# Float32r products of 12-bit parts for scores and queries in a latent-attention layer

## The chip, the core and the metric

The kernel runs on one core of a Trainium2 chip, as one launch. The metric is the device time in microseconds of that launch, the median of several runs. The core has a matrix engine (TensorE, PE in the profile, with its weight loads as PEld), three engines for elementwise work (VectorE or DVE, ScalarE or ACT, GpSimd or POOL), and SyncE (SP), from whose queue nearly all transfers are issued. Matmul results land in PSUM, from where DVE and ACT read them.

## What is computed

One transformer layer on 8 sequences of 512 tokens with 512 features: attention with latent queries and keys (16 heads), then a gated feed-forward block. Cut to what matters:

```python
x = hidden                                        # (8, 512, 512)
a = layernorm(x)
q = rmsnorm(a @ wq_a.T, q_norm_w)                 # latent of 384
q = (q @ wq_b.T).reshape(b, s, 16, 128 + 64)      # per head: q_nope 128, q_pe 64
kv = a @ wkv_a.T
kv_c = rmsnorm(kv[..., :128], kv_norm_w)          # latent of 128
k_pe = rope(kv[..., 128:])                        # 64, shared by all heads
k_nope, v = split(kv_c @ wkv_b.T)                 # per head 128 and 128
scores = (concat(q_nope, rope(q_pe)) @ concat(k_nope, k_pe).T) / sqrt(192)
out = softmax(scores) @ v
x = x + out @ wo.T
y = layernorm(x)
x = x + ((silu(y @ e4m3(gate_w) * gs) * (y @ e4m3(up_w) * us)) @ e4m3(down_w)) * ds
```

All inputs and the output are float32.

## The kernel before

**Folding.** The key projection is folded into the query weights and the value projection into the output weights. `fold_q(h)` multiplies a head's `wqn` and `wkn` and keeps the product, scaled by both norm weights, in SBUF (`wa0` to `wa3`, four heads each); `sum_q` adds the sums of weight blocks that Strassen's scheme needs. So scores need only the 128-wide latent of the keys, and no keys or values per head are made. `fold_o` does the same for the output; those weights go to scratch memory and come back for each later sequence (`wst`).

**Per sequence.** `latents(b)` normalizes the tokens, projects them with `wlr` (a Strassen scheme of its own, `project_two_x`), and transposes the result into `lat`: three blocks of 128 rows of query latent and one of key latent, by 512 tokens. `kpe` holds the rotary keys as two float32r parts, a rounded one and the remainder.

**Per pair of heads.** `project_pe` makes the rotary queries of two heads with three 128x512 float32 matmuls (`qpe_ps`, L659), applies the rotation (`rope`, L442 to L445) and splits the result into float32r parts in `qpe`. `project_two` makes the latent queries `qn` of two heads by a Strassen scheme over the two heads and the two halves of the tokens: eleven 128x256 float32 matmuls (L746) in four stages, with halves copied and added by ACT and DVE (L760 to L782). The first pair is done by `project`, with six full matmuls (L692).

**Per head, four steps.** One step is one `scores(b, h, t)`: 128 queries against 512 keys. One float32 matmul with the latent (L793) and two float32r matmuls with the rotary parts (L795) add into one PSUM tile `sc`. DVE takes the negated maximum `nmax` (L797), ACT the exponential with its sum `den` (L800). One step later DVE inverts `den` (L803) and ACT scales (L804); another step later DVE transposes 32x32 blocks (L169). Every two steps `send` writes the blocks to scratch memory (`way`, L179) and reads them back as the full transpose `prT` (L183). `attend` multiplies `prT` with the values' latent `kvt` (L814), six steps after the last score of its head. `sums` and `output` form the output product of four heads by another Strassen scheme (L860) and add it to `x` on DVE (L864).

**Order.** All of this is written out by hand: `steps` lists the (sequence, head, tile) steps in order, `work[i]` holds what is issued in step `i` beside the scores, and `put(i, f)` adds to it; `at(b, h, t)` gives a step's number. Every engine runs its own instructions in that order. `put_q` places the query projections, 4 to 6 steps before the head that needs them. In each step the loop first issues the transpose of the step before last, then the inverse and the scaling of the last step, then the scores, maximum and exponential of this one, then `work[i]`. While attention runs, the feed-forward weights are rounded to e4m3 in pieces (L73 to L84) and stored.

**PSUM.** The ring `ps_r` has 5 buffers of 128x512 float32, used by `sc`, `av`, projections and transposes in turn; `ps_q` has one for Strassen's sums, `ps_o` two for output products.

**Feed-forward.** It runs after attention, with float32r throughout: `y` and the gated result are split into two parts, and each product takes two matmuls (L267, L1188).

Of the kernel before, what the change touches and what calls it, by code (L numbers as in the profile page):

```python
# [45 lines left out]
P = 128  # L46
# [3 lines left out]
NH = 16  # L50
# [12 lines left out]
RL = RQ + RKV + DR  # L63

# [24 lines left out]
class Layer:  # L89
    def __init__(self, ctx, tc, ins, out):  # L90
# [4 lines left out]
        self.ps_r = ctx.enter_context(tc.tile_pool(name="ps_r", bufs=5, space=PSUM))  # L95
# [4 lines left out]
        self.wlr = self.wp.tile([P, NC, RL], F32, tag="wlr", name="wlr")  # L100
# [7 lines left out]
        self.size = {"wg": 3, "wu": 6, "wd": 4}  # L108
# [8 lines left out]
        ]  # L117

# [16 lines left out]
    def ln_stats(self, x, small):  # L135
# [3 lines left out]
        st = small.tile([P, NT, 6], F32, tag="ln_st", name="ln_st")  # L139
        mv = small.tile([P, NT, 2], F32, tag="ln_mv", name="ln_mv")  # L140
        sd = small.tile([P, NT], F32, tag="ln_sd", name="ln_sd")
        rstd = small.tile([P, NT], F32, tag="ln_rstd", name="ln_rstd")
# [61 lines left out]
    def ffn_parts(self):  # L204
        return (
            self.xp.tile([P, NC, S], F32R, tag="lat", name="yh", bufs=2),
            self.wp.tile([P, NC, S], F32R, tag="wlr", name="yl"),
        )

    def ffn_normed(self, x, small, psum, work):  # L210
# [3 lines left out]
        yh, yl = self.ffn_parts()  # L214
        *stats, mv, rstd = self.ln_stats(x, small)
# [16 lines left out]
    def ffn_normed_blocks(self, x, y, small, work):  # L232
# [3 lines left out]
        yh, yl = self.ffn_parts()  # L236
# [39 lines left out]
    def attention(self):  # L276
        tc, nc, ins, wp, xp = self.tc, self.nc, self.ins, self.wp, self.xp
        with ExitStack() as ctx:
# [4 lines left out]
            ps_q = ctx.enter_context(tc.tile_pool(name="ps_q", bufs=1, space=PSUM))  # L283
# [20 lines left out]
            wlr_sums = wp.tile([P, 3, 2, RL // 2], F32, tag="wlr_sums", name="wlr_sums")  # L304
# [10 lines left out]
            nc.gpsimd.tensor_scalar(knr, knr, SCALE, None, ALU.mult)  # L315
            cs_s = None
            wqp_s, wa_s, wst_s = [], [], {}
# [9 lines left out]
            def load_pe(g):  # L327

                wqp = self.load_w(f"wqp{g}", ins["wqp"][g])
                wqp_s.append(wqp)  # L330

                def times():
                    for r in range(NR):
                        nc.gpsimd.tensor_scalar(
                            wqp[:, r, :], wqp[:, r, :], qnw[:, r : r + 1], None, ALU.mult
                        )

                return times
# [8 lines left out]

            def fold_q(h):


                fold_q_products(h)()

            def fold_q_products(h):

                g, j = divmod(h, G)
# [15 lines left out]

                return evict

            def sum_q(pair):

# [886 lines left out]
```

## Time and profile before

| | |
|---|---|
| median of 3 runs | 2683.82 us (2683.11 to 2685.96) |
| span of the profiled execution | 2680.7 us, 30590 instructions |
| profiled execution's own time beside its span | not given by the page; the median is 3.1 us above the span |
| granted TensorE clock | 1.000 of full speed |
| transfers | 433.51 MB, mean 162 GB/s |
| first and last score matmul | 38.9 and 2127.7 us |

The profile is of one execution. Its page gives the busy time of each engine, the span in 40 slices, and groups of instructions by line, engine and tile, with the mean time of one and the idle time of the engine just before them with what ended it. Matmuls overlap in their pipeline and their ends are modelled, so the distance from one start to the next says what a matmul costs. A float32 matmul of the program leaves two records, a float32r matmul one.

### The profile page before, as it was taken

What the parts mean: (1) busy time and instruction counts of PE and PEld (TensorE: products, weight loads), DVE (VectorE), ACT (ScalarE), POOL (GpSimd) and SP (SyncE); (2) the same over time, 40 slices, a digit from 0 to 9 for tenths busy, and PEclk for the clock granted to TensorE, in tenths of its full rate; (3) what the DMA queues carried; (4) which work ended last, traced back from release to release, by engine and by line L of the source; (5) the groups of instructions that cost most, each with busy time, mean ns of one, the idle gap of its engine ahead of it and who ended that gap; (6) DMA issues with size and microseconds to landing.
All of it is one profiled execution on the core that took longest, in us unless ns stands there. A gap on an engine that the chain in (4) does not pass through costs nothing.

```text
span 2680.7 us, 30590 instructions
## 1 busy us (share of the span) xinstructions
PE 2668.3 (100%) x9782; PEld 1820.0 (68%) x9782; DVE 1506.2 (56%) x3369; ACT 1272.8 (47%) x2675; POOL 655.9 (24%) x754
## 2 busy tenths in 40 slices
PE   9999999999999999999999999999999999999999
PEld 5566666666666666666666666666666688888887
DVE  5655566656666666566666666666555543333332
ACT  4454554555455545555545454555555433333332
POOL 3342222222222222222222222222111122222222
PEclk9999999999999999999999999999999999999999
DMA  4665565555655555565555555655565641111110
GB/s 124 219 197 172 173 202 182 180 178 187 188 178 179 198 180 177 181 205 176 174 192 187 181 171 189 204 173 167 183 213 190 204 159 65 63 64 66 64 63 20
DMA packets 266561, 433.51 MB, mean 162 GB/s; under 512 B 30112, under 2 KB 193312, under 8 KB 264864
## 3 DMA queue, kind: packets, MB, share of 16 engines
q1 hardware_dynamic: 262080, 426.64, 49.0%
q10 hardware_dynamic: 4320, 4.92, 0.7%
q8 instruction: 78, 1.28, 0.2%
q14 instruction: 83, 0.68, 0.1%
HBM read 256.33 MB, written 175.11 MB: 161 GB/s over the span
## 4 chain that ended last, share of the span: by engine, by line
PE 92%; ACT 3%; DVE 3%; DMA 1%; issue 0%; SPq 0%; ACTq 0%; POOL 0%; DVEq 0%; POOLq 0%
PE av L814 16%; PE sc L793 14%; PE sc L795 8%; PE u_ps L860 7%; PE pd L1188 7%; PE pg L267 6%; PE qn_two L746 6%; PE pu L267 6%; PE qpe_ps L659 6%; PE v_ps L860 4%; PE qn_ps L746 3%; PE z_ps L860 2%; PE lr_u L548 2%; PE lr_z L548 1%; DMA way<-block 1%; ACT pr L804 1%
## 5 line engine op out<-in xcount | busy, mean ns | idle before, releaser
L804 ACT ACTIVATE pr<-pr,den 128x512 f32<-128x512 f32 x512 | 369.9, 722 | 658.0 <-DVE den L803 652.5
L797 DVE TENSOR_REDUCE nmax<-sc 128x1 f32<-128x512 f32 x512 | 347.8, 679 | 317.0 <-PE sc L795 315.7
L795 PE MATMUL sc<-kpe,qpe 128*128 128x512 f32 x1024 | 525.8, 594 | 0.0
L793 PE MATMUL sc<-lat,qn 128*128 128x512 f32 x1024 | 523.0, 592 | 0.5 <-ACT qn L776 0.5
L814 PE MATMUL av<-prT,kvt 128*128 128x512 f32 x1024 | 460.5, 592 | 0.6 <-issue 0.3
L800 ACT ACTIVATE pr<-sc,nmax 128x512 f32<-128x512 f32 x512 | 346.7, 677 | 157.1 <-DVE nmax L797 156.8
L169 DVE STREAM_TRANSPOSE block<-pr 128x512 f32<-128x512 f32 x512 | 359.4, 702 | 16.6 <-DMA way<-block 12.5
L795 PEld LDWEIGHTS sc<-kpe,qpe 128*128 128x128 f32 x1024 | 194.5, 190 | 244.9 <-issue 244.1
L814 PEld LDWEIGHTS av<-prT,kvt 128*128 128x128 f32 x1024 | 193.7, 189 | 196.2 <-issue 185.5
L445 POOL TENSOR_TENSOR roped<-roped,rope_sw 128x512 f32<-128x512 f32 x72 | 91.7, 1274 | 809.0 <-DVE rope_sw L444 792.7
L793 PEld LDWEIGHTS sc<-lat,qn 128*128 128x128 f32 x1024 | 192.2, 190 | 78.9 <-issue 45.5
L1171 POOL TENSOR_TENSOR fl<-fuse,fh 128x512 fp32r<-128x512 f32 x96 | 126.5, 1318 | 381.9 <-ACT fh L1170 381.9
L1167 DVE SCALAR_TENSOR_TENSOR fuse<-pu,us,gate 128x512 f32<-128x512 f32 x96 | 71.9, 750 | 193.9 <-PE pu L267 189.0
L659 PE MATMUL qpe_ps<-lat,wqp 128*128 128x512 f32 x384 | 175.3, 592 | 0.7 <-issue 0.7
L1188 PE MATMUL pd<-wd,fh 128*128 128x512 f32 (+1 forms) x396 | 150.5, 383 | 0.0
L1188 PE MATMUL pd<-wd,fl 128*128 128x512 f32 (+1 forms) x396 | 150.5, 383 | 0.0
L267 PE MATMUL pu<-yh,wu 128*128 128x512 f32 x384 | 150.1, 391 | 0.4 <-ACT gate L1165 0.4
L267 PE MATMUL pg<-yh,wg 128*128 128x512 f32 x384 | 150.0, 391 | 0.0
L78 POOL TENSOR_TENSOR raw<-raw,q_m 128x256 f32<-128x256 f32 x72 | 63.9, 887 | 349.7 <-DVE q_m L76 349.7
L267 PE MATMUL pu<-yl,wu 128*128 128x512 f32 x384 | 149.4, 389 | 0.0
L267 PE MATMUL pg<-yl,wg 128*128 128x512 f32 x384 | 149.4, 389 | 0.0
L1165 ACT ACTIVATE gate<-pg,gs 128x512 f32<-128x512 f32 x96 | 66.0, 689 | 174.0 <-PE pg L267 173.5
(169 smaller groups left out, 4162.0 us busy)
## 6 DMA issues: line engine op xcount, KB each, us to landing
way<-block SPq DMA_DIRECT2D x256, 512.0 KB, 3.1
prT<-way SPq DMA_DIRECT2D x1024, 128.0 KB, 2.8
wst<-wst_d SPq DMA_DIRECT2D x56, 512.0 KB, 4.5
wst<-wst_d SPq DMA_DIRECT2D x56, 384.0 KB, 3.9
x<-in_hid SPq DMA_DIRECT2D x60, 256.0 KB, 3.4
x<-x SPq DMA_DIRECT2D x16, 512.0 KB, 4.4
out<-o SPq DMA_DIRECT2D x31, 256.0 KB, 2.0
wst_d<-wst SPq DMA_DIRECT2D x8, 896.0 KB, 4.6
```

The source lines that it names most:

```text
L169: self.nc.vector.transpose(out[:, :, :, i : i + Q].rearrange("p c k i -> p k c i"), x.rearrange("p (k c j) -> p k c j", c=NQ, j=Q),)
L267: self.nc.tensor.matmul(ps, self.ffn_w[name, i][:, c * P : (c + 1) * P], y[k][:, c, :], start=c == 0 and k == 0, stop=c == NC - 1 and k == 1,)
L659: nc.tensor.matmul(ps, wqp_s[g][:, r, pj * P : (pj + 1) * P], lat[:, r, :], start=r == 0, stop=r == NR - 1)
L746: nc.tensor.matmul(to, m, n, start=start and k == 0, stop=stop and k == len(terms) - 1, skip_group_check=True,)
L793: nc.tensor.matmul(sc, qn[:, q], lat[:, NR, :], start=True, stop=False)
L795: nc.tensor.matmul(sc, qpe[:, h % 2, q], kpe[:, part, :], start=False, stop=part == 1)
L797: nc.vector.tensor_reduce(nmax, sc, AX.X, ALU.max, negate=True)
L800: nc.scalar.activation(pr, sc, AF.Exp, bias=nmax, accum_out=den)
L804: lambda: nc.scalar.activation(pr, pr, AF.Identity, scale=den),
L814: nc.tensor.matmul(av, kvt[:, kt, :], prT[:, :, :, kt, :], start=kt == 0, stop=kt == NT - 1)
L860: nc.tensor.matmul(got[name][:, t, :], ops[p][left][:, t * P : (t + 1) * P], w[:, p, right, :], start=first and t == 0 and p == 0, stop=la ...
L1188: nc.tensor.matmul(pd, f[:, i, t * P : (t + 1) * P], w["wd", i][:, cols], start=i == 0 and f is fh, stop=i == NI - 1 and f is fl,)
```

## The change

- Scores: `qn` and the key latent (`latk`) are each kept as three float32r parts: a rounded high part, the remainder, and a difference of the two. The float32 matmul L793 becomes three float32r matmuls. They go into two PSUM tiles: `mid` takes the product of the differences and the two rotary products (L763, L765), `sc` the products of the high parts and of the remainders (L767). ACT copies `mid` to `pr` with a scale (L771), DVE adds `sc`, scales and takes the minimum in one instruction (`tensor_tensor_reduce`, L773), and the exponential reads the result with scale -1.
- Query projections: latent queries and rotary queries of a pair of heads are made by the same function `project_q`, nine float32r matmuls for each of three outputs (L703, L710), again in two PSUM tiles, joined by an ACT copy (L707) and a DVE instruction (L714). `project_two`, `sum_q`, `sum_latents` and the Strassen halves are gone. `project` splits `qn` into parts on ACT, POOL and DVE (L722 to L724).
- The query weights' three parts are made once, in the first sequence (`weight_parts`), stored to scratch memory (`wq_d`), and loaded again for each pair of each later sequence, in three pieces; a ring of two buffers holds them.
- The query latent's parts (`latq`, one buffer) come from `transpose_q`; the key latent has its own `transpose_kv`.
- `ps_r` has 6 buffers, and `ps_q` is gone. The first product of the query's rotation moves from DVE to POOL (L457). The reading back of `prT` is issued one turn later. In the loop, the scaling of the last step (`between`) is issued on ACT between the copy of `mid` and the exponential. The output's third step is cut in two, and some work is placed in other steps. The rotary cast L681 is gone; the second difference goes to DVE as two 64-row instructions (L750, L751). Gate weights are loaded in two pieces of six.

The diff, cut to its core:

```diff
-        self.ps_r = ctx.enter_context(tc.tile_pool(name="ps_r", bufs=5, space=PSUM))
+        self.ps_r = ctx.enter_context(tc.tile_pool(name="ps_r", bufs=6, space=PSUM))
...
+            def weight_parts(p, j, w4, engine=nc.gpsimd):
+                parts = wq_s[0, p]
+                hi, lo, mid = (parts[:, k, :, j * P : (j + 1) * P] for k in range(3))
+                nc.scalar.activation(mid, w4, AF.Identity, scale=DOWN)
+                nc.scalar.activation(hi, w4, AF.Identity, scale=DOWN * T)
+                engine.tensor_tensor(lo, w4, mid, ALU.subtract)
+                engine.tensor_tensor(mid, hi, lo, ALU.subtract)
...
+            def load_wq(b, p):
+                def piece(k):
+                    if k == 0:
+                        wq_s[b, p] = wp.tile([P, 3, NR, 3 * P], F32R, tag="wq", name="wq", bufs=2)
+                    nc.sync.dma_start(wq_s[b, p][:, k].bitcast(F32), self.wq_d[p][:, k].bitcast(F32))
...
+                    hi, lo, mid = (latq[0][:, k, :, t * P : (t + 1) * P] for k in range(3))
+                    nc.scalar.activation(hi, pt, AF.Identity, scale=DOWN)
+                    nc.vector.tensor_tensor(lo, pt, hi, ALU.subtract)
+                    nc.vector.scalar_tensor_tensor(mid, hi.bitcast(F32), -ONE_T, pt, ALU.mult, ALU.add)
...
+            def project_q(b, pair, k):
+                w = wq_s[b, pair]
+                latq = state["latents", b][0][0]
+                cols = slice(k * P, (k + 1) * P)
+                ps, mid = (ps_r.tile([P, S], F32, tag="r", name=n) for n in ("q_ps", "q_mid"))
                 for r in range(NR):
                     nc.tensor.matmul(
-                        ps, wqp_s[g][:, r, pj * P : (pj + 1) * P], lat[:, r, :], start=r == 0, stop=r == NR - 1
+                        mid, w[:, 2, r, cols], latq[:, 2, r, :], start=r == 0, stop=r == NR - 1
                     )
+                q = hp.tile([P, S], F32, tag="qa", name="qa", bufs=2)
+                nc.scalar.copy(q, mid)
+                for part in range(2):
+                    for r in range(NR):
+                        nc.tensor.matmul(
+                            ps, w[:, part, r, cols], latq[:, part, r, :],
+                            start=part == 0 and r == 0, stop=part == 1 and r == NR - 1,
+                        )
+                nc.vector.scalar_tensor_tensor(q, ps, ONE_T, q, ALU.mult, ALU.add)
+                return q
...
+                def parts():
+                    qn = state["qn", b, h] = hp.tile([P, 3, S], F32R, tag="qn", name="qn")
+                    nc.scalar.activation(qn[:, 0, :], q, AF.Identity, scale=DOWN)
+                    nc.gpsimd.tensor_tensor(qn[:, 1, :], q, qn[:, 0, :], ALU.subtract)
+                    nc.vector.scalar_tensor_tensor(
+                        qn[:, 2, :], qn[:, 0, :].bitcast(F32), -ONE_T, q, ALU.mult, ALU.add
+                    )
...
-                sc = ps_r.tile([P, S], F32, tag="r", name="sc")
-                nc.tensor.matmul(sc, qn[:, q], lat[:, NR, :], start=True, stop=False)
+                mid, sc = (ps_r.tile([P, S], F32, tag="r", name=n) for n in ("mid", "sc"))
+                nc.tensor.matmul(mid, qn[:, 2, q], latk[:, 2, :], start=True, stop=False)
                 for part in range(2):
-                    nc.tensor.matmul(sc, qpe[:, h % 2, q], kpe[:, part, :], start=False, stop=part == 1)
+                    nc.tensor.matmul(mid, qpe[:, h % 2, q], kpe[:, part, :], start=False, stop=part == 1)
+                for part in range(2):
+                    nc.tensor.matmul(sc, qn[:, part, q], latk[:, part, :], start=part == 0, stop=part == 1)
...
-                nc.vector.tensor_reduce(nmax, sc, AX.X, ALU.max, negate=True)
-                nc.scalar.activation(pr, sc, AF.Exp, bias=nmax, accum_out=den)
+                nc.scalar.activation(pr, mid, AF.Identity, scale=1.0 / ONE_T)
+                between()
+                nc.vector.tensor_tensor_reduce(
+                    pr, sc, pr, scale=-ONE_T, scalar=3.0e38, op0=ALU.add, op1=ALU.min, accum_out=nmax
+                )
+                nc.scalar.activation(pr, pr, AF.Exp, bias=nmax, scale=-1.0, accum_out=den)
...
                         def turned(i=i, blocks=blocks, block=block, prT=prT, t=t):
+                            while on_way and i < len(steps) - 2:
+                                on_way.pop(0)()
                             blocks()
                             if t % 2:
                                 on_way.append(self.send(prT[:, t // 2], block))
-                                while i != len(steps) - 3 and on_way:
-                                    on_way.pop(0)()
+                            while on_way and i == len(steps) - 1:
+                                on_way.pop(0)()
```

## The prediction

> **What bounds the kernel now.** I read the page first: the busy shares and the 40 slices.
>
> ```profile
> PE 2668.3 (100%) x9782; PEld 1820.0 (68%) x9782; DVE 1506.2 (56%) x3369; ACT 1272.8 (47%) x2675; POOL 655.9 (24%) x754
> ```
>
> TensorE is busy for the whole span. The windows view says whether that holds in both stages; after the window come PE, weight loads, DVE, ACT, POOL, the granted clock, the DMA share and GB/s.
>
> ```profile
> 820.00:1080.00 260.00, 259.79 (x896) 167.74 (x895) 161.68 (x377) 136.40 (x298) 63.77 (x77) 1.00 0.58 186
> 2158.00:2681.00 523.00, 518.72 (x2311) 430.12 (x2309) 195.03 (x340) 163.44 (x270) 126.45 (x96) 1.00 0.20 70
> ```
>
> In attention (scores start from 38.9 to 2127.7 us, so 261 us a sequence and 4.08 us for each of its 64 score steps) PE leaves 0.2 us idle in 260; DVE is at 62%, ACT at 52%, POOL at 25%. A busy PE is no proof of necessary work, so I need the price of each matmul. Durations of pipelined matmuls overlap (rows say 592 ns), so prices are start-to-start. The chain of waits, cut to a stretch where it stays on PE, adds them up:
>
> ```profile
> 1005.72 0.86 PE qn_two L746 x4
> 1006.58 0.86 PE qn_ps L746 x4
> 1007.44 0.86 PE sc L793 x2
> 1008.30 0.47 PE sc L795 x2
> 1008.77 3.44 PE av L814 x8
> 1013.53 2.58 PE qpe_ps L659 x6
> ```
>
> Each float32 matmul leaves two records: one 128x512 product costs 0.86 us, one 128x256 half 0.43. The float32r pair L795 is one record each: 0.47 for two. The feed-forward stage, all float32r, in the timeline gives the steady price: 54 matmuls between these two starts, 12.23 us, 0.2265 each, each with its own weight load and at clock 1.00.
>
> ```profile
> 2299.66 0.39 PE L267 MATMUL pg<-yl,wg 128*128 128x512 f32 x1
> ...
> 2311.89 0.39 PE L267 MATMUL pg<-yl,wg 128*128 128x512 f32 x1
> ```
>
> So three float32r products cost 0.68 against 0.86. The other engines' prices are in the groups by form:
>
> ```profile
> L804 ACT ACTIVATE pr<-pr,den 128x512 f32<-128x512 f32 x512 | 369.9, 722 | 658.0 <-DVE den L803 652.5 <-DMA wo<-in_wo 2.5 <-issue 2.2
> L800 ACT ACTIVATION_READ_ACCUMULATOR pr<-sc,nmax 128x1 f32 x512 | 97.9, 191 | 0.0
> L817 ACT COPY o<-av 128x512 f32<-128x512 f32 x128 | 74.8, 585 | 142.7 <-PE av L814 142.7
> L673 ACT CAST qpe<-roped 128x512 fp32r<-128x512 f32 x64 | 39.6, 619 | 0.3 <-POOL roped L445 0.3
> L797 DVE TENSOR_REDUCE nmax<-sc 128x1 f32<-128x512 f32 x512 | 347.8, 679 | 317.0 <-PE sc L795 315.7 <-DVE den L803 0.3
> L803 DVE RECIPROCAL den<-den 128x1 f32<-128x1 f32 x512 | 63.6, 124 | 5.5 <-ACT pr L800 5.5
> L444 DVE SCALAR_TENSOR_TENSOR rope_sw<-rope_sw,cs 128x512 f32<-128x512 f32 x72 | 49.4, 687 | 0.0
> L641 POOL TENSOR_TENSOR kpe<-roped,kpe 128x512 fp32r<-128x512 f32 x8 | 10.2, 1277 | 1.1 <-ACT kpe L640 1.1
> ```
>
> The long idle entries of ACT and DVE end on each other or on PE: they have room, but each step hands work back and forth.
>
> **PE's part.** Scores: in each of 512 steps one float32 matmul (0.86) becomes three float32r (0.68): -0.1805 x 512 = -92.4 us. Queries: a pair of heads had three rotary matmuls (2.58) and eleven Strassen halves (11 x 0.432 = 4.75), together 7.33; now it has 27 float32r matmuls, 6.12. That is -1.21 x 63 = -76.5, and the first pair, which had nine full matmuls (7.74), gains 1.6. Transposes, attention products, output products and feed-forward keep their counts. Sum: -170.5 us. The granted clock is 1.00 in every window, the all-float32r ones included, so I take no slower matmul. Break-even would be a float32r price of 0.28 us.
>
> **ACT's part.** Each step gains a copy of `mid` out of PSUM (by L817, 585 ns; 512 of them, 299.5 us); each head and pair a copy of `q_mid` (192, 112.3) and each head a rounding to float32r (128 by L673, 79.4). The four half copies of a pair (63 x 4 at 0.3625, 91.4) and one of three rotary casts (39.6) go. Weight parts, first sequence only, add about 48 x 0.47 = 23 (between the 256- and 512-wide copies). Net +383, or +45 for a later sequence: 136 + 45 = 181 of 240 us, 76%.
>
> **DVE's part.** The reduce becomes an add-and-minimum over PSUM and SBUF that also writes its output, plus an accumulator read. No row shows it. Its nearest row is the reduce, 0.68; the two-input reads of PSUM (L864, 0.687) agree. The accumulator read lies between DVE's one-column reciprocal (0.124) and ACT's read (0.191). I take 0.81 in all; the lower bound is 0.68, no read at all; the upper bound is two passes, 2 x 0.679 + 0.191 = 1.55. New: 192 joins of `ps` and `mid` (132.5), 128 third parts of q (by L444, 88), smaller latent parts (40), one more rotary half (43); +66 for the reduce. Gone: 106 for the halves, 43 for the rope product that moves to POOL. Net +221, 27.6 a sequence: 190 of 240, 79%.
>
> One rule speaks against this: the Trainium skill's page "Vector Engine (DVE) Microarchitecture Reference", section "Points that are easy to get wrong", says that a scalar-tensor-tensor with two non-bf16 sources in SBUF runs at half throughput. L444 is that form and took 687 ns, against 674 ns for L443 with a PSUM source, so here the row decides. By the rule the third parts of q would cost about 0.65 us more each, an estimate: 10 us of DVE a sequence.
>
> **POOL's part.** 128 second parts of q (1.28 each by L641, 164), 64 rope products (82), weight and latent parts, less Strassen's sums: about +30 a later sequence, 95 of 240 or 40%. Its results are used a step or more later, 3.75 us, which covers 1.28; without that cover PE would wait up to 1.3 us for each of 128 heads, 164 us.
>
> **Transfers.** Query weights no longer stay resident: 168 loads of 576 KB, 99 MB, in sequences 2 to 8. At the 186 GB/s now moved, 14 MB a sequence lifts the rate to about (48 + 14) MB in 240 us, 260 GB/s. Each load costs SP about 0.4 us of issue, and is queued ahead of `way` and `prT`; the first use comes 9 steps after the first piece (34 us) and 5 after the last (19), against landings of 4 to 5 us for 384 to 512 KB, so it is hidden. `prT` is now issued one turn later, so that SP does not sit on `way`'s landing (787.8 us today); attention products still start six steps after the scores, 22.5 us. From scores to `prT` I count two steps and a transpose (8.2), landing 3.1, issue 1.7, landing 2.8: 16 us. Doubling both landings still fits; nothing, or at most 2 us a head (256 us), which I keep for the range only.
>
> **New waits.** A step's chain is copy 0.585, reduce 0.81, exponential 0.68 and its read 0.19, with 0.04 at each hand-over (the reduce ended at 1006.44, the exponential began at 1006.48): 2.35 us, against 3.75 of PE on average. In ACT's queue the exponential now waits for a reduce that itself waits for a copy just ahead of it; behind it stand the copies that free PE's banks. The old scaling L804 fills most of that gap. The ring `ps_r` has six buffers for 24 tiles in eight steps, two steps of lead, where it had five for about 13, three steps. Some steps carry only a score (1.13 us of PE), and ACT gets two table loads of 1.283 us around each square root; then PE can catch up with its ring. Between 0 and 6 us a sequence, I take 2: 17 us in all, nearer to none, because ACT and DVE both keep a fifth of their time.
>
> **Start.** Before the first score come eight latent-part instructions on DVE (0.55 each, by the 384-wide row L469, 4.4 us), two POOL steps for the key latent and one for q (3 x 1.28); 0 to 12, I take +8.
>
> **Sum.** Span 2680.7 - 170.5 + 8 + 17 = 2535.2. The page gives no total of the profiled run beyond its span; the median of 2683.8 lies 3.1 above that span, so the forecast is 2538 us.
>
> **The rivals.** *ACT and DVE pace the steps.* For it: 76 and 79% busy with a chain each step, and a ring with a third less lead. Against it: 0.7 us of slack a step. If PE waits 0.1 to 0.3 us a step, 51 to 154 us replace the 17: 2572 to 2675.
>
> *Slower: the fused reduce takes two passes* (L773, every step). At 1.55 us DVE's 190 becomes 237 of 240, and with some 0.25 us a step of waiting for copies and reads about 253; 5% more where joins of q bunch makes 265, 25 a sequence above PE's 240, 200 us in place of the 17: about 2721. It decides from about 1.5 us. For it: a second input, an output and an accumulator in one instruction, unseen here. Against it: L864, L444 and L1167, the two-input forms, all took 0.68 to 0.75.
>
> *The price does not carry over:* if float32r matmuls cost 0.28 in attention, as when weight loads (0.19 each) do not hide, the result is no change. Against it: the pair L795 already runs at 0.23.
>
> **How the numbers follow.** The forecast case, PE still the bound (2509 to 2565), 0.57; steps paced by ACT and DVE, 0.30; no change 0.02; slower 0.11. The range 2508 to 2612 holds the first and a little over half of the second. A difference of 0.2%, 5 us, is about what can be told from none: faster 0.87, same 0.02, slower 0.11.
>
> **What would show it.** Right: L763 and L767 starts 0.23 apart, PE near 100% in windows of sequences 2 to 8, the score step at 3.75 to 3.85 us, DVE near 79%, the feed-forward stage still 523 us. Wrong: idle time ahead of `mid` or `q_mid` on PE released by DVE or ACT (the ring), ahead of `av` released by a DMA, or an L773 row far above 0.7 us.

## The result: slower, and the profile after

The changed kernel takes 2754.4 us (median of four runs, 2752.8 to 2758.0) against 2683.5 us beside it: a ratio of 1.0266, with an interval from 1.0251 to 1.028. The forecast was 2538. The profiled execution has a span of 2752.4 us, so 71.7 us were lost where 145 were expected to be won.

The page of the changed kernel: busy time by engine, then PE's busy share and its granted clock in 40 slices.

```profile
PE 2582.6 (94%) x10240; PEld 1911.8 (69%) x10240; DVE 1778.6 (65%) x4021; ACT 1605.5 (58%) x3245; POOL 1005.7 (37%) x943
PE   7899899989998999899999998999999999999999
PEclk8999999999999999999999999999999999999999
```

PE was at 100% and has gaps now, nearly all in the attention stage. The windows view shows the same two stages as before.

```profile
820.00:1080.00 260.00, 239.89 (x926) 173.19 (x927) 192.34 (x444) 167.97 (x348) 98.78 (x93) 0.99 0.75 229
2230.00:2752.00 522.00, 518.62 (x2289) 426.24 (x2287) 200.51 (x337) 161.54 (x269) 125.99 (x96) 1.00 0.20 69
```

In 260 us of attention PE idles for 20 us, and more than that shows when its work is priced. I priced every matmul of the traces start to start, as the prediction did (0.2266 us for a float32r matmul, 0.429 for each of the two records of a 128x512 float32 product). In all, the matmuls come to 2650.7 us before and 2481.9 after: 168.8 us less, where the prediction took 170.5. But from the first score to the last attention product PE spends 16.5 us more than its prices before and 239.1 us more after. That is the whole result: -167 for the matmuls of that stretch, +223 for time in which PE stood or ran slowly, +12 for a later first score (38.9 to 50.7 us), +4 behind the last attention product.

No engine is full, however. The groups by form show what the instructions cost:

```profile
L773 DVE CUSTOM_DVE_ANT_0 pr<-sc,pr 128x512 f32<-128x512 f32 x512 | 345.2, 674 | 72.3 <-ACT pr L771 69.9 <-PE mid L765 0.3
L773 DVE DVE_READ_ACCUMULATOR2_ANT nmax<- 128x1 f32 x512 | 42.0, 82 | 0.0
L771 ACT ACTIVATE pr<-mid 128x512 f32<-128x512 f32 x512 | 300.2, 586 | 75.5 <-PE mid L765 75.2 <-issue 0.2
L714 DVE SCALAR_TENSOR_TENSOR qa<-q_ps,qa 128x512 f32<-128x512 f32 x192 | 132.8, 692 | 279.7 <-ACT qa L707 249.3 <-PE q_ps L710 20.1 <-issue 8.9
L724 DVE SCALAR_TENSOR_TENSOR qn<-qn,qa 128x512 fp32r<-128x512 f32 x128 | 119.0, 930 | 148.5 <-ACT qn L722 147.4
```

The fused reduce took 0.674 us and its accumulator read 0.082, together 0.756: one pass. The durations are as predicted; the new part is the idle time at the end of the lines. Before, the largest wait of DVE in attention was for PE (316 us, L797 in the prediction). The waits view, DVE's and then PE's (us in total, times, longest):

```profile
DVE qa L714 <- ACT qa L707: 249.3, 178, 1.9
DVE qn L724 <- ACT qn L722: 147.4, 74, 3.7
DVE pr L773 <- ACT pr L771: 69.9, 117, 3.2
...
PE u_ps L836 <- DVE x L620: 24.4, 12, 2.4
PE q_mid L703 <- ACT pr L771: 18.7, 9, 2.2
PE av L790 <- ACT pr L771: 16.2, 18, 1.3
PE mid L763 <- DVE qn L724: 15.7, 13, 2.0
PE sc L767 <- DVE nmax L773: 14.2, 20, 1.3
```

DVE waits for ACT, 467 us in these three rows alone, and each of PE's five largest rows names one of the two. The rows of `q_mid` and `av` behind L771 and of `sc` behind L773 are waits for a bank of the ring `ps_r`, which that instruction frees; `mid` behind L724 waits for its operand. The timeline shows one turn of it (start, duration, in brackets the idle time ahead and its end):

```profile
855.57 1.62 PE L703 MATMUL q_mid<-latq,wq 128*128 128x512 f32 x3 [2.15 <-ACT pr L771]
856.98 2.40 PE L710 MATMUL q_ps<-latq,wq 128*128 128x512 f32 x6
...
857.56 0.57 ACT L771 ACTIVATE pr<-mid 128x512 f32<-128x512 f32 x1
...
858.04 0.71 ACT L780 ACTIVATE pr<-pr,den 128x512 f32<-128x512 f32 x1
858.17 0.69 DVE L773 CUSTOM_DVE_ANT_0 pr<-sc,pr 128x512 f32<-128x512 f32 x1 [0.32 <-ACT pr L771]
...
858.91 0.72 ACT L776 ACTIVATE pr<-pr,nmax 128x512 f32<-128x512 f32 x1 [0.16 <-DVE nmax L773]
...
859.63 0.57 ACT L707 COPY qa<-q_mid 128x512 f32<-128x512 f32 x1
860.23 0.69 DVE L714 SCALAR_TENSOR_TENSOR qa<-q_ps,qa 128x512 f32<-128x512 f32 x1 [1.36 <-ACT qa L707]
```

The copy L707 of `q_mid` stands behind the exponential L776 in ACT's queue; the exponential waits for DVE's reduce L773; and next in DVE's queue is the join L714, which waits for L707. So DVE stands for exponential, read and copy, 1.36 us here and 1.40 on average over 178 times. The third part L724 does the same behind the rounding L722, for 74 of the 128 heads. The six matmuls at 856.98 show something else: 2.40 us, where six of them took 1.52 at 1007.71. They ran at half clock: the granted clock was 0.5 from 855.4 to 858.8 us, around the end of a wait of PE of 2.15 us.

### The profile page after: what moved, and what is told of

Its sections match the earlier page's. It is cut to its first block, busy times and chain, and to the rows that moved or that the text cites. A ratio compares the mean times of both kernels' runs of the same rounds, so it can differ in the third digit from the quotient of the medians.

```text
span 2752.4 us, 34226 instructions
## 1 busy us (share of the span) xinstructions
PE 2582.6 (94%) x10240; PEld 1911.8 (69%) x10240; DVE 1778.6 (65%) x4021; ACT 1605.5 (58%) x3245; POOL 1005.7 (37%) x943
## 4 chain that ended last, share of the span: by engine, by line
PE 31%; DVE 7%; ACT 6%; DMA 3%; issue 3%; SPq 1%; POOL 0%; DVEq 0%; ACTq 0%
PE pu L272 6%; PE pd L1178 6%; PE pg L272 6%; PE av L790 3%; DVE block L175 2%; ACT pr L776 2%; PE u_ps L836 2%; PE q_ps L710 2%; ACT pr L780 2%; DMA way<-block 1%; PE mid L765 1%; PE sc L767 1%; PE q_mid L703 1%; PE v_ps L836 1%; DVE pr L773 1%
## 5 line engine op out<-in xcount | busy, mean ns | idle before, releaser
L773 DVE CUSTOM_DVE_ANT_0 pr<-sc,pr 128x512 f32<-128x512 f32 x512 | 345.2, 674 | 72.3 <-ACT pr L771 69.9
L776 ACT ACTIVATE pr<-pr,nmax 128x512 f32<-128x512 f32 x512 | 364.5, 712 | 12.3 <-DVE nmax L773 9.2
L767 PE MATMUL sc<-latk,qn 128*128 128x512 f32 x1024 | 323.6, 396 | 26.2 <-DVE nmax L773 14.2
L771 ACT ACTIVATE pr<-mid 128x512 f32<-128x512 f32 x512 | 300.2, 586 | 75.5 <-PE mid L765 75.2
L765 PE MATMUL mid<-kpe,qpe 128*128 128x512 f32 x1024 | 319.6, 393 | 6.2 <-DVE qpe L751 6.2
L723 POOL TENSOR_TENSOR qn<-qa,qn 128x512 fp32r<-128x512 f32 x128 | 213.5, 1668 | 306.0 <-ACT qn L722 305.5
L714 DVE SCALAR_TENSOR_TENSOR qa<-q_ps,qa 128x512 f32<-128x512 f32 x192 | 132.8, 692 | 279.7 <-ACT qa L707 249.3
L710 PE MATMUL q_ps<-latq,wq 128*128 128x512 f32 x1152 | 306.6, 403 | 0.3 <-DVE nmax L773 0.3
L763 PE MATMUL mid<-latk,qn 128*128 128x512 f32 x512 | 278.5, 544 | 21.8 <-DVE qn L724 15.7
L710 PEld LDWEIGHTS q_ps<-latq,wq 128*128 128x128 f32 x1152 | 226.9, 197 | 51.5 <-DVE nmax L773 0.9
L767 PEld LDWEIGHTS sc<-latk,qn 128*128 128x128 f32 x1024 | 188.8, 188 | 85.4 <-DVE nmax L773 24.9
L765 PEld LDWEIGHTS mid<-kpe,qpe 128*128 128x128 f32 x1024 | 192.7, 189 | 63.3 <-issue 29.0
L82 POOL TENSOR_TENSOR raw<-raw,q_m 128x256 f32<-128x256 f32 x72 | 64.7, 898 | 442.0 <-DVE q_m L80 437.3
L724 DVE SCALAR_TENSOR_TENSOR qn<-qn,qa 128x512 fp32r<-128x512 f32 x128 | 119.0, 930 | 148.5 <-ACT qn L722 147.4
L703 PE MATMUL q_mid<-latq,wq 128*128 128x512 f32 x576 | 177.7, 418 | 34.6 <-ACT pr L771 18.7
```

The lines of the kernel that those rows point to most:

```text
L710: nc.tensor.matmul(ps, w[:, part, r, cols], latq[:, part, r, :], start=part == 0 and r == 0, stop=part == 1 and r == NR - 1,)
L723: nc.gpsimd.tensor_tensor(qn[:, 1, :], q, qn[:, 0, :], ALU.subtract)
L763: nc.tensor.matmul(mid, qn[:, 2, q], latk[:, 2, :], start=True, stop=False)
L765: nc.tensor.matmul(mid, qpe[:, h % 2, q], kpe[:, part, :], start=False, stop=part == 1)
L767: nc.tensor.matmul(sc, qn[:, part, q], latk[:, part, :], start=part == 0, stop=part == 1)
L771: nc.scalar.activation(pr, mid, AF.Identity, scale=1.0 / ONE_T)
```

## The experiments

Two numbers stand beside each run: what PE lost against its prices from the first score to the last attention product, and for how much of that stretch the granted clock was 0.5, both from the trace. Five kernels were run once (e_ring5, e_one_sum, e_q_only, e_scores_only, e_early_start), three twice (e_order_nopool, e_order_one_sum, e_order3_dve), the others four to ten times; runs of one kernel lie within 3.5 us of each other, those of the changed kernel within 5.2, of e_q_late within 6.7 and of e_early_warm within 9.8. The kernel before, run again beside each group, took 2682.0 to 2683.7 us.

| run | us | PE lost | at half clock |
|---|---|---|---|
| before | 2683.5 | 16.5 | 0 |
| after | 2754.4 | 239.1 | 75.1 |
| e_ring5 | 2754.3 | 237.0 | 44.4 |
| e_one_sum | 2722.1 | 206.9 | 102.4 |
| e_q_only | 2702.0 | 95.9 | 54.6 |
| e_scores_only | 2693.0 | 75.8 | 27.3 |
| e_q_late | 2683.3 | 81.9 | 27.3 |
| e_early | 2698.5 | 181.8 | 92.2 |
| e_early_warm | 2683.8 | 169.4 with dummies | 54.6 |
| e_early_start | 2663.9 | 146.8 | 47.8 |
| e_order2 | 2653.6 | 138.7 | 81.9 |
| e_order | 2631.4 | 116.4 | 30.7 |
| e_order_nopool | 2625.9 | 110.6 | 44.4 |
| e_order3_dve | 2628.2 | 112.7 | 34.1 |
| e_order3 | 2621.8 | 106.4 | 23.9 |
| e_order_one_sum | 2589.7 | 72.7 | 27.3 |

Theory A: the order of ACT's and DVE's queues, in which a head's work for q stands behind the step's exponential and reduce, holds PE. Rival B: the PSUM ring `ps_r` is too short for its new tiles. Rival C: DVE and POOL block each other.

**The ring with five buffers.**

```diff
-        self.ps_r = ctx.enter_context(tc.tile_pool(name="ps_r", bufs=6, space=PSUM))
+        self.ps_r = ctx.enter_context(tc.tile_pool(name="ps_r", bufs=5, space=PSUM))
```

> The changed kernel with five instead of six buffers in ps_r. Theory A: PE's lead is not what limits, 2750 to 2785. Theory B: a sixth of the lead gone where the lead is the limit, 2830 or more. Theory C: as A.

2754.3 us, no difference, where B expected 2830 or more: the number of buffers is not what holds PE. The ring is not free of cost, though. PE's largest wait is now for a bank:

```profile
PE av L790 <- DVE nmax L773: 34.3, 27, 2.7
```

In the changed kernel that row is 2.0 us. What the waits added was about made up by 31 us less at half clock (worth at most 15 us, an estimate at half speed), so a sixth of the ring may be worth some 13 us; the equal times hide that by luck. A longer ring was not run.

**One PSUM sum for the scores**, with the old reduction and exponential, without copy, fused reduce and the scale between the sums.

```diff
-                mid, sc = (ps_r.tile([P, S], F32, tag="r", name=n) for n in ("mid", "sc"))
+                sc = ps_r.tile([P, S], F32, tag="r", name="sc")
...
-                nc.scalar.activation(pr, mid, AF.Identity, scale=1.0 / ONE_T)
                 between()
-                nc.vector.tensor_tensor_reduce(
-                    pr, sc, pr, scale=-ONE_T, scalar=3.0e38, op0=ALU.add, op1=ALU.min, accum_out=nmax
-                )
-                nc.scalar.activation(pr, pr, AF.Exp, bias=nmax, scale=-1.0, accum_out=den)
+                nc.vector.tensor_reduce(nmax, sc, AX.X, ALU.max, negate=True)
+                nc.scalar.activation(pr, sc, AF.Exp, bias=nmax, accum_out=den)
```

> All five score matmuls add into one PSUM tile without the scale between the two sums (so the scores are not the reference's); the copy of mid and the fused reduce give way to the old reduce and the exponential from PSUM. PE's matmuls, the query projections and their joins stay. Ring demand falls from 24 to 16 tiles in eight steps, ACT loses 0.58 us a step. Theory A: the waits of the joins behind the exponential stay (1.36 us each), the step's chain loses the copy: 2640 to 2720. Theory B: the ring has its old three steps of lead, 2540 to 2590. Theory C: 2740 or a little less.

2722.1 us. This is 2 us above A's range and far from B's. 300 us of ACT's copies and a third of the ring's tiles are gone, and only 32 us come back: neither ACT's busy time nor the ring is the limit. The two waits of q stay about as they were, as the waits view of this run shows:

```profile
DVE qa L714 <- ACT qa L707: 232.2, 168, 1.9
DVE qn L724 <- ACT qn L722: 172.2, 74, 5.1
```

**The work for q issued ahead of the step's scores.** PE's query matmuls, ACT's copy L707, its rounding and POOL's second part go ahead of the step's copy and exponential; DVE's join and third part stay behind the reduce. Nothing else changes.

```diff
-                put(i + n, plain)
+                early[i + n].append(plain)
...
+                        while early[i]:
+                            early[i].pop(0)()
                         inverse, times, blocks = scores(b, h, t, block, times or (lambda: None))
```

> Same arithmetic; in each step the query matmuls, ACT's copy of q_mid and ACT's and POOL's parts of qn are issued ahead of the step's scores, while DVE's join (L714) and third part (L724) stay behind the reduce, so that neither waits for an ACT instruction queued behind the exponential. Theory A (DVE's queue sets the pace: about 200 us busy plus 62 us waiting for ACT in each sequence of 273): L714's 249 us and L724's 147 us of waiting nearly vanish, PE idles less, 2560 to 2640 us. Theory B (the ring of six PSUM buffers for 24 tiles in eight steps sets the pace): the demand on the ring is the same, 2735 to 2765. Theory C (DVE and POOL block each other): also unchanged, 2735 to 2765.

2698.5 us (ratio to before 1.0061, 1.0045 to 1.0078): 56 us better by order alone. The time lies between the ranges: above A's (2560 to 2640) and below that of B and C. So the order matters, as A says, but not to the extent expected. The waits of L714 and L724 vanish; DVE now waits for the copy of `mid` behind the same ACT work, and PE at a few single places:

```profile
DVE pr L775 <- ACT pr L773: 422.3, 301, 7.8
...
PE q_mid L703 <- issue: 32.0, 7, 4.6
PE u_ps L838 <- DVE x L620: 30.0, 12, 2.8
```

The first PE row is the start of each later sequence; the view names no releaser, but at 845.24 us `q_mid` starts 0.1 us after the last L657 ends. `latq` has one buffer, so its four transposes follow the last head's projection; each passes through ACT and twice through DVE (L655 to L657) before `q_mid` of the next sequence can start. The old kernel had one copy there. The second is the bank that DVE frees late after the latents' products.

**Each half of the change alone.** First q in float32r and the scores in one float32 sum as before:

```diff
-                nc.tensor.matmul(mid, qn[:, 2, q], latk[:, 2, :], start=True, stop=False)
+                nc.tensor.matmul(sc, qn[:, q], latk, start=True, stop=False)
```

> Only the query projections are float32r; scores are one float32 matmul and two float32r in one tile, with the old reduce and exponential, and qn needs no parts. By PE's prices 2683.5 - 78 + 5 = 2611. Theory A: DVE has 24 joins a sequence that wait for ACT, but no third parts and no fused reduce; its queue has room: 2605 to 2640. Theory B: 14 tiles in six buffers, the same, 2605 to 2630. If it is far above, the projections alone carry the loss.

2702.0 us, far above either expectation. PE idles for 56 us in attention, and half of that is one row, seven times at a sequence's start:

```profile
PE q_mid L698 <- issue: 27.5, 7, 4.2
```

The loss was about 10 us for each later sequence, more than twice the 3.9 us of the wait. Then the scores from parts, with q as three float32 matmuls in one sum:

```diff
+                        ps, w[:, 0, r, cols].bitcast(F32), latq[:, 0, r, :].bitcast(F32), start=r == 0, stop=r == NR - 1
```

> The other half of the change: scores as three float32r products in two sums with the copy and the fused reduce, but q as three float32 products of 128x512 in one PSUM sum, copied out by ACT (no joins, no third or second parts of weights and latents); each head still makes its three parts of q. PE: 512 x 0.18 less, a pair of heads 7.74 in place of 7.33: 2683.5 - 92 + 26 = 2617 us without any new wait. Theory 'the queues' ping-pong per head costs the most' (third part L724 waits for ACT behind the exponential): 2650 to 2700. Rival 'the join L714 alone is the wait': 2617 to 2635.

2693.0 us, in the range of the theory named first: its third part of q waits for ACT (225 us; the copy of `mid` is waited for longer, 248). Its largest row on PE is 18.1 us, seven waits of up to 2.8 us at a later sequence's start, for `qpe`. So each half alone loses its gain: q 79 us more on PE than before, against 78 gained; the scores 59 against 66, and 17 us at the start and behind the last product. Neither is "the" cause, and together they lose 223, more than 79 and 59: the losses of the halves don't simply add.

**A sequence's start reordered.** The transposes take three steps in place of four, and the first rotary projection comes one step later; first on the kernel with float32r for q alone, then on e_early.

```diff
-                    first = b > 0 and h == 0
+                    first = 2 * (b > 0 and h == 0)
...
-                    put(at(b - 1, 13, 2) + t, p["transpose_q"], t)
+                    put(at(b - 1, 13, 2) + (t + 1) // 2, p["transpose_q"], t)
```

> Only q in float32r, scores in one float32 sum, and the start of a sequence reordered: the four transposes of the query latents take three steps instead of four, and the first rotary projection of a sequence is issued one step later. In the run without the reordering PE idled 4.1 us once a sequence ahead of that projection, and the loss against the sum of matmul prices was 9.5 us a sequence with the half-clock stretch that followed. Theory 'waits at one place, doubled by the clock gate': the loss goes, 2702 - 7 x (6 to 9.5) = 2636 to 2660, faster than before, and the row q_mid <- issue of 27.5 us vanishes. Rival 'the engines beside PE set the pace': the wait moves to the next place that needs DVE or ACT, 2690 to 2702.

2683.3 us (1.0003, 0.9994 to 1.0012): 19 us better, less than half of the expectation. The wait ahead of `q_mid` is gone, and a new one of 2.2 us ahead of the rotary matmul of the scores has come (15.9 us in all), probably because the parts of `qpe` are now made one step before their use.

> The kernel with ACT's and PE's query work issued ahead of the step's scores (2698.5 us), and in addition the same reordering of a sequence's start. There PE idled 4.74 us at each of seven starts, followed by half-clock stretches of 3.4 or 6.8 us. Theory 'waits at few places, doubled by the clock gate': 2698 - 7 x (6 to 8) = 2642 to 2656. Rival 'ACT and DVE set the pace': 2685 to 2698, with the wait at another line.

2663.9 us, 35 us better, again short of the expectation (2642 to 2656) but clearly not the rival's (2685 or more).

**Products spaced**, on top of that: a pair's last piece of latents one step earlier, the output product's first matmuls one step later.

```diff
-                        for n, f in zip((0, 2, 3, 5), p["project_two_x"](pair)):
+                        for n, f in zip((0, 2, 3, 4), p["project_two_x"](pair)):
...
-                        when = (8, 12, 16, 16, 17, 17, 19) if late else (8, 12, 15, 16, 17, 17, 19)
+                        when = (8, 12, 16, 16, 17, 17, 19) if late else (9, 12, 15, 16, 17, 17, 19)
```

> As the kernel before it, and the output product's first matmuls one step later, the last piece of a pair's latents one step earlier, so that DVE has three steps in place of one to free the bank that u_ps waits for (2.6 us, twice a sequence, each followed by a half-clock stretch of 3.4 us). Theory 'waits at few places, doubled by the clock gate': another 7 x 2 x (2.6 + 1.7) = 60 us at most, 2585 to 2630, faster than before by 2 to 3.5%. Rival 'ACT and DVE set the pace': within 15 us of the kernel without this step, 2640 to 2690.

2631.4 us, just above the theory's range, and a ratio to before of 0.9807 (0.979 to 0.9823): the same arithmetic as the slower kernel, 123 us faster, all by order. The windows view for the stretch of above:

```profile
820.00:1080.00 260.00, 253.68 (x1007) 186.78 (x1006) 199.68 (x481) 184.15 (x377) 102.81 (x100) 1.00 0.80 248
```

DVE does more in 260 us than after (199.7 against 192.3 us), ACT too (184.2 against 168.0): neither was at its limit there.

**What an idle PE costs.** In e_early, PE stands 4.6 us at a sequence's start. The windows view of that run, around the wait at 840.7 (the clock is the third number from the end):

```profile
840.70:845.20 4.50, 0.00 (x0) 0.00 (x0) 2.69 (x8) 2.77 (x6) 0.00 (x0) 1.00 0.60 189
845.60:848.80 3.20, 3.20 (x9) 2.52 (x8) 1.68 (x6) 1.90 (x4) 0.00 (x0) 0.50 1.06 289
849.00:853.00 4.00, 4.00 (x20) 3.45 (x19) 1.39 (x3) 2.02 (x4) 0.00 (x0) 1.00 1.04 388
```

Nine matmuls in 3.2 us, then twenty of about the same price in 4.0: the wait is followed by 3.4 us at half clock. To see whether that costs time, useless work was put into the wait, and nothing else was changed:

```diff
+                if b and pair == 0 and k == 2:
+                    for n in range(36):
+                        nc.tensor.transpose(mid[:, n % NT * P : n % NT * P + P], self.ident, self.ident)
```

> The kernel with the query work issued ahead (2698.5 us) and, at each of seven sequence starts where PE idles 4.7 us for the last query latents, 36 transposes of the identity into the bank of q_mid, which the next matmul overwrites: useless work of about 3.9 us in the idle time. The waits and all results stay as they are. Theory 'an idle PE costs twice, since the granted clock falls to half for 3.4 or 6.8 us afterwards': the half-clock stretches at the starts go, 7 x (1.7 to 3.4) = 12 to 24 us less, 2675 to 2687. Rival 'the half clock is only a mark in the records and costs nothing beside the wait': 2697 to 2703.

2683.8 us, 14.7 us less than e_early and in the expected range: 252 more matmuls made the kernel faster. Half-clock time fell by 37.6 us, which at half speed is worth 18.8 (an estimate). The timeline of this run at the same place:

```profile
839.01 4.12 PE L704 MATMUL q_mid<-ident 128*128 128x128 f32 x36
843.62 0.97 PE L706 MATMUL q_mid<-latq,wq 128*128 128x512 f32 x3 [0.49 <-DVE latq L657]
844.43 1.55 PE L713 MATMUL q_ps<-latq,wq 128*128 128x512 f32 x6
```

The six matmuls of `q_ps` take 1.55 us here and 2.70 in e_early.

**A miss that shows the same.** The transposes another step earlier, the rotary projection back at its old step.

```diff
-                    put(at(b - 1, 13, 2) + t, p["transpose_q"], t)
+                    put(at(b - 1, 13, 1) + (t + 1) // 2, p["transpose_q"], t)
```

> As the reordered kernel that took 2631.4 us, but the transposes of the query latents another step earlier and the first rotary projection of a sequence back at its old step, so that its last parts are made two steps ahead of their use in place of one (there mid waited 1.73 us for qpe once a sequence). Theory 'waits at few places': 7 x (1.7 to 3.4) = 12 to 24 us less, 2607 to 2620. Rival 'DVE's queue there is simply full': the wait moves to the neighbouring place (sc <- DVE qa, 1.93 us), 2625 to 2640.

2653.6 us (0.9887, 0.987 to 0.9903), 22 us worse than e_order, outside both expectations. The wait went to the neighbouring place, as the rival said, but it now comes in one piece of 2.9 us, with 2.1 us more in the 5 us behind it. It comes in each sequence but the last, six times ahead of the transposes for the next one and in the first sequence ahead of L406, each time with 6.8 us at half clock:

```profile
1072.60:1079.20 6.60, 5.75 (x14) 4.03 (x14) 4.74 (x12) 4.36 (x11) 0.77 (x1) 0.50 0.26 99
```

Half-clock time grew by 51 us, at half speed worth 26 (an estimate); PE's loss grew by 22. With half of the half-clock time taken off, the two orders lose about the same (101 and 98 us).

**POOL beside DVE.** e_order without POOL's two additions of the weight rounding, 144 instructions by the page's counts (not the 192 of the expectation):

```diff
-    nc.gpsimd.tensor_tensor(r, w, m, ALU.add)
-    nc.gpsimd.tensor_tensor(r, r, m, ALU.subtract)
```

> The reordered kernel (2631.4 us) without the two POOL additions of the rounding of the feed-forward weights (L82 and L83 there, 192 of them; that part of the rounding is left out). Theory 'DVE's instructions with two SBUF inputs are slowed by POOL's work beside them' (L753 1.10 us beside POOL and 0.69 without): those rows fall to 0.69 where these additions were beside them, DVE has some 60 to 100 us less, and the waits for it shrink: 2600 to 2622. Rival 'those instructions are long for another reason': rows unchanged, 2628 to 2635.

2625.9 us, 5.5 us less and between the two. Of the rows, the third part of q fell from 840 to 778 ns and the later half of the second difference of `qpe` (L753 in e_order) from 1057 to 982; the sum of DVE fell by 17 us. Contention is there, and what these additions add to it is worth little; most of POOL's work, the second part of q beside the third one too, was left, so the whole of it is not measured.

**Two sums against one, in the better order.** The edit of e_one_sum on e_order:

> The reordered kernel (2631.4 us) with all five score matmuls in one PSUM sum, the old reduction and the old exponential (the scale between the two sums is left out). This takes the copy of mid and its wait (DVE L775 <- ACT L773, 368 us in 305 places) out of every step. Theory 'the copy in ACT's queue is what still holds DVE and then PE': 2590 to 2612. Rival 'those waits of DVE are cover, PE's loss sits elsewhere (first sequence 28 us more than the later ones, single places)': 2620 to 2632.

2589.7 us (0.9647, 0.9628 to 0.9667), just below the theory's range. DVE follows PE again:

```profile
DVE nmax L774 <- PE sc L769: 218.5, 128, 9.1
```

So in this order the second sum costs 42 us: the copy and its hand-over, the fused reduce in place of the old one, and a third of the ring's tiles, which this run doesn't separate. Whether the copy's place in ACT's queue matters was the next question: the same instructions as in e_order, with ACT's work for q moved behind the step's copy of `mid`, into the time in which ACT waits for the reduce.

```diff
+                        def between(i=i, times=times):
+                            if times:
+                                times()
+                            while after[i]:
+                                after[i].pop(0)()
+
-                        inverse, times, blocks = scores(b, h, t, block, times or (lambda: None))
+                        inverse, times, blocks = scores(b, h, t, block, between)
```

> The reordered kernel (2631.4 us), with ACT's copies of q_mid, its casts of the rotary q and its rounding of q moved in ACT's queue from ahead of a step's copy of mid to behind it, into the time in which ACT waits for the fused reduce. Same instructions, same matmul order. Theory 'the place of the copy of mid in ACT's queue holds DVE, and that PE': most of the 42 us that the copy costs there goes, 2592 to 2612, and the wait DVE <- ACT of 368 us falls below 200. Rival 'the copy itself, one more hand-over in each step': 2625 to 2640, since the exponential is now late instead and with it the banks that the copies free.

2621.8 us (0.9764, 0.9747 to 0.978), the fastest kernel here that does all of the arithmetic. DVE's wait for the copy fell from 368 to 237 us, but the time by 10 only, between the two ranges and nearer to the rival's. So the move is worth a quarter of the 42 us. The copy's place may be worth more than that, since the move slowed something else:

```profile
L725 DVE SCALAR_TENSOR_TENSOR qn<-qn,qa 128x512 fp32r<-128x512 f32 x128 | 143.2, 1119 | 18.1 <-ACT qn L720 16.5
```

The third part of q took 840 ns in e_order and takes 1119 here, 36 us more of DVE. What the rest of the 42 us is, the copy itself, the other parts of the second sum or this, stays open.

**The first sequence.** In e_order, PE loses 44.6 us in the first eighth of attention, about 10 in each later one. With the splitting of folded weights on DVE instead of POOL (`evict()` with `nc.vector`):

> As the kernel just before, and the two subtractions that split each folded head's weights (28 subtractions of 128x384 in the first sequence) on DVE instead of POOL. Theory 'PE waits for POOL's splitting in the first sequence' (q_mid <- POOL wq, 16.4 us, and half-clock stretches after): 10 to 20 us below the kernel just before. Rival 'the first sequence is slow for DVE and ACT, which fold there too': within 5 us of it or up to 15 us slower.

2628.2 us, 6 us slower, as the rival said. PE's waits for POOL fell from 17.7 to 8.2 us and came back elsewhere. Which engine would have to be relieved there stays open.

## Why the prediction was wrong

**The step that failed is "New waits".** It took 17 us, with at most 6 us a sequence; PE lost 223. It argued that ACT and DVE "both keep a fifth of their time" and that a step's chain of 2.35 us fits into PE's 3.75. Both held: ACT was busy for 65% and DVE for 74% of the window, and the chain's four instructions take 2.24 us (0.586, 0.756, 0.712, 0.186). Neither decides. What it left out is that a head's work for q crosses between ACT and DVE three more times, in queues where each of these instructions stands behind one that waits for the other engine. The prediction even wrote that the exponential waits for a reduce that waits for a copy just ahead of it, and that the copies which free PE's banks stand behind it; it then priced only the chain of a step that has nothing else in it. Its own first sign of being wrong is there: `q_mid` and `mid` wait for ACT and DVE (18.7 and 15.7 us in the largest rows). Reordering the same instructions gave back 123 of the 216 us between forecast and result (e_early, e_early_start, e_order).

**"New waits" had no term for the clock.** The prediction took the granted clock as 1.00 because every window before had it, but before, PE hardly stood (0.2 us in 260). After, 75 us of attention ran at half clock. At half speed that is worth at most 38 us, an estimate, and less where another engine sets the pace. e_early_warm shows that it costs, and e_order2 that it can decide between two orders.

**"ACT and DVE pace the steps"** was the right kind of rival, at 0.1 to 0.3 us a step; PE lost 0.44 (223 over 512 steps). It named the chain, the busy shares and the ring's shorter lead as its grounds; a step's chain and the lead were not what decided (e_ring5, e_early). The chance of 0.11 for slower hung on two passes of the fused reduce, which did not happen; a slower result from ordinary durations had no rival of its own.

**PE's part** was right: 168.8 us against 170.5, L767 starts 0.227 apart, the feed-forward stage 522 us. So was the price that carries over.

**ACT's and DVE's parts** were right in size. A score step takes 4.17 us after, so a sequence 267 us; scaled to that, the window gives DVE 197 us (predicted 190), ACT 172 (181) and POOL 101 (95). Within POOL's part, the second part of q took 1.67 us instead of 1.28. Within DVE's part, the fused reduce was 0.756 instead of 0.81, and the third part of q 0.93 instead of 0.69. The rule about two SBUF sources that the prediction weighed is not seen where nothing runs beside it: in e_order, 23 of the 128 third parts of q met no POOL work and took a median of 692 ns; the 41 that lay beside POOL for over nine tenths of their time took 1132.

**Transfers** were right: PE waited 3 us for `prT`, although its landing rose from 2.8 to 3.7 us. **Start** was 12 instead of 8, and the first sequence as a whole was not priced: some 35 us more than a later one even in the better order.

From the best time without the second sum, 2589.7, to the forecast of 2538, 52 us remain. The first sequence's extra (38.5 us in the first eighth there, 4 to 5 in each later one but the last, 9 in that), 4 us of start and 4 behind the last attention product are most of it; what makes up the last of these, and the first sequence's extra, stays open.

## What to carry to other kernels

A busy share of 60 to 80% is no reserve when two engines hand work back and forth in fixed queues: before pricing waits, write down each engine's queue for one full turn and mark every instruction that stands behind one which waits for the other engine. Issue what is ready (copies that another engine needs) ahead of what waits, and look at each place where a single-buffered tile is refilled once per outer loop. And where the matrix engine was never idle, its full clock is part of the old time: waits of 2 us put that at risk as well.

## What the runs showed of the hardware

**Half clock after short waits.** In the changed kernel, between 300 and 2080 us, 14 stretches ran at a granted clock of 0.5, each for 3.4 or 6.8 us, and each came with 2.1 to 4.7 us of waits of PE, counted against its prices in pieces of over 0.4 us from 8 us ahead of the stretch on, with the wait during which it began. Waits of 1.93 and 0.93 us within 4 us, once a sequence in e_order, were followed by none. Nor does the same wait always do it: in the changed kernel, `u_ps` waits 2.3 to 2.4 us once a sequence for L620, and a half clock came with this wait at 971.8, 1243.9 and 1516.7 us, and none at 433.1, 702.4 and 1787.7. All changes of the clock in this trace lie whole multiples of 3.413 us apart, so where in such a grid a wait falls may decide; that is not shown. The runs give no sharp threshold. The Trainium skill's page "TensorE: Matmul & The Clock Gate", section "HAM oscillation — how this bites in real kernels", gives the rule to have no idle gaps of PE over about 3.4 us; the lengths of the stretches agree with its window, but here no single wait ahead of these stretches was longer than 2.5 us, so by these traces a shorter wait is enough.

**DVE beside POOL.** The timeline of e_order:

```profile
1054.93 0.69 DVE L752 TENSOR_TENSOR qpe<-roped,qpe 64x512 fp32r<-64x512 f32 x1
1054.98 1.24 POOL L82 TENSOR_TENSOR raw<-raw,q_m 128x256 f32<-128x256 f32 x1 [0.56 <-DVE q_m L80]
1055.66 1.11 DVE L753 TENSOR_TENSOR qpe<-roped,qpe 64x512 fp32r<-64x512 f32 x1
1056.30 1.05 POOL L83 TENSOR_TENSOR raw<-raw,q_m 128x256 f32<-128x256 f32 x1
```

Two DVE instructions of the same form: the one that started just ahead of POOL's took 0.69 us, the one that started while POOL's ran took 1.11. In the same run L88 (two SBUF inputs) took 0.43 us alone and 0.90 beside POOL, while L714, with one input in PSUM, took 0.68 in both cases. Of the third parts of q in e_order, the 60 that started while a POOL instruction ran took a median of 1130 ns, the 45 that started ahead of one 684. L753 took what was left of POOL's instruction (0.56 us in the median beside L82) plus 0.55. The Trainium skill's page "SBUF — State Buffer", section "SBUF: two separate sides", says that DVE with two SBUF inputs and GpSimd take an exclusive lock on a shared pair of ports, and that whichever starts first keeps it for its whole instruction; these rows and medians agree with it.
